# A graph network on one core: loads between layers 0 and 1 that wait for rows of y

## The chip, the cores and the metric

The kernel runs on one core of one Trainium2 chip. The metric is device time in microseconds, from launch to end, as the median of several runs. Times inside a run come from one profiled execution and are counted from the start of its span.

## The reference

2708 nodes with 512 features each pass through four layers. Each layer normalises the features (LayerNorm), computes something over the adjacency matrix and adds it to x. Layer 0 is a weighted mean over neighbours. Layer 1 is an attention whose mask is so strong that the kernel reduces it to a choice of one row: for each node, the row of the projected matrix y that the largest entry of the node's adjacency row points to. Layer 2 is a two-step graph convolution and layer 3 a mean over neighbours.

```python
h = relu(layernorm(x));  x = x + layer0(h, adj)
h = relu(layernorm(x));  x = x + layer1(h, adj)        # here: x1 + y[idx]
h = relu(layernorm(x))
h = relu(adj @ (h @ W1) + b1)
h = relu(adj @ (h @ W3) + b3)
x = x + tanh(h @ Wf + bf)
h = relu(layernorm(x));  x = x + (adj != 0) @ (h @ W + b) / deg
```

## The kernel before

Nodes are cut into 22 tiles of 128 rows (the last has 20). Matrices are split into high, low and shifted parts, so that each product in layer 2 is three products at the fast float32 rate. The adjacency is treated as dense in its first six column tiles; beyond them, each node tile has a list of the neighbours that occur, and the rows of those are gathered by indirect transfers. Only node tile 0 reads the whole adjacency column.

Layer 0 leaves two things in device memory: x1, its output in tiles, and y, the projected rows that layer 1 picks from. The core then opens the passage to layer 2. `fetch(t)` (L1034) loads tile t of x1 on SyncE's queue and gathers the rows `y[idx]` on GpSimd's queue; slots are there for nine tiles (AHEAD, L1032), and nine fetches are issued at the start (just above L1074). `first_product(t)` (L1047) adds the two, stores x2, normalises, calls `fetch(t + 9)`, transposes and splits (`relu_parts`, L871), multiplies by W1 (`project3`, L889), and stores the product in g1d. The main loop of this step (L1077) goes over node tiles m. For each, `aggregate` (L943) loads its list (`load_listed`, L926), gathers listed rows of g1d, and loads pieces of three adjacency tiles (`load_piece`, L915) that are marked (L953) and split by ScalarE (L971) and VectorE (L972, L973). For m = 0 the pieces cover all 22 tiles, and calling for their parts is what drives `first_product` through t = 0 to 21. The gathers of g1d for m = 1 need all 22 products stored.

Weights pass through one raw buffer `wr`: W3 is split from it right after the nine fetches (L1074), Wf is loaded into it at once (L1075), and inside the loop at m = 0 it is split into the space of W1, and W is loaded. The biases b1 and b3 are loaded ahead of the fetches (L1027, L1028).

The order on each engine isn't the order of the program text. The framework's scheduler places every instruction by its own idea of durations, and semaphores carry the dependences. Each engine then works through its list strictly in order, SyncE's and GpSimd's transfer issues included. So where an instruction stands is fixed when the kernel is built, and one that waits holds all that stand behind it on its engine.

A helper `behind(dst, last)` existed in layer 0 only: it copies one element on VectorE from a tile into the buffer that a load is about to fill. The load overwrites that buffer and so can't be issued before the copy, and the copy can't run before its source is there.

Of the kernel before, what the change touches and what calls it, by code (L numbers as in the profile page):

```python
# [9 lines left out]
FP = mybir.dt.float32  # L10
# [12 lines left out]
P = 128  # L23
# [19 lines left out]
def kernel(  # L43
# [27 lines left out]
    nc = tc.nc  # L71

    N, D = x.shape
    H, _, DK = wk_d.shape
    NT = (N + P - 1) // P
    NFULL = N // P
# [10 lines left out]
    def rows(t):  # L87
        return min(P, N - t * P)

    def dense_of(m):  # L90

        return 0 if m == NT - 1 else DENSE
# [59 lines left out]
    def span(t):  # L152
        return slice(t * P, t * P + rows(t))

    def project(acc, hT, n, w):

        for c in range(NCD):
            nc.tensor.matmul(  # L158
                acc[:n], hT[:, c, :n], w[:, c, :], start=(c == 0), stop=(c == NCD - 1)
            )  # L160

    def load_w(pool, src, name, first=None):
        w = pool.tile([P, NCD, D], FP, name=name)
        if first:
            first(w)
        nc.sync.dma_start(out=w, in_=src.rearrange("(c p) k -> p c k", p=P))
        return w
# [23 lines left out]
    def split_b(hi, lo, s, v, scale=1.0):  # L191

        nc.scalar.activation(hi, v, AF.Copy, scale=UP * scale)
        if scale == 1.0:
            nc.vector.tensor_tensor(lo, v, hi.bitcast(FP), ALU.subtract)
        else:
            nc.vector.scalar_tensor_tensor(
                lo, v, scale, hi.bitcast(FP), op0=ALU.mult, op1=ALU.subtract
            )
        nc.vector.scalar_tensor_tensor(  # L200
            s, lo.bitcast(FP), SHIFT, hi.bitcast(FP), op0=ALU.mult, op1=ALU.add
        )
        nc.scalar.activation(lo, lo.bitcast(FP), AF.Copy, scale=-SHIFT)

    def split_w(pool, raw, tag):

        w = [pool.tile([P, NCD, D], FR, name=f"{tag}{i}") for i in range(3)]
        for c in range(NCD):
            split_b(*(part[:, c, :] for part in w), raw[:, c, :])
        return w  # L210

    short = ctx.enter_context(ExitStack())
    wset = short.enter_context(tc.tile_pool(name="wset", bufs=1))
# [6 lines left out]
    with tc.tile_pool(name="l0_slab", bufs=2) as slabs, tc.tile_pool(  # L220
        name="l0_h", bufs=1
    ) as hp, tc.tile_pool(name="l0_w", bufs=2) as wp, tc.tile_pool(
        name="l0_acc", bufs=2, space=PSUM
    ) as ps_acc, tc.tile_pool(name="l0_small", bufs=1, space=PSUM) as ps_small, tc.tile_pool(
        name="l0_list", bufs=3, space=PSUM
    ) as ps_list, tc.tile_pool(name="l0_tr", bufs=1, space=PSUM) as ps_tr, tc.tile_pool(
        name="l0_y", bufs=1, space=PSUM
# [189 lines left out]
        def norm_h0(ts):  # L417
            for t in ts:
                n = rows(t)
                norm(wp, h0[t], n, h0[t], AF.Relu)  # L420
                nc.gpsimd.dma_start(out=h0d[span(t)], in_=h0[t][:n])

        def behind(dst, last):

            nc.vector.tensor_copy(dst, last)

        wv = wset.tile([P, NCD, D], FP, name="wa0")
        wo = wset.tile([P, NCD, D], FP, name="wa1")
# [49 lines left out]
        masks, row, slab = {}, {}, {}  # L478
# [277 lines left out]
        incs, hns, xs = {0: incidence(0)}, {}, {}  # L756
# [9 lines left out]
        for m in range(NT):  # L766
# [45 lines left out]
            if m == NT // 2 + 6:  # L812
                wr = load_w(wset, w1_d, "wr", lambda w: behind(w[:1, 0, :1], xt[:1, :1]))
                w1 = split_w(wset, wr, "wa")
                wr = load_w(wset, w3_d, "wr")
# [12 lines left out]
    gp = short.enter_context(tc.tile_pool(name="g", bufs=1))  # L828
    wsetb = short.enter_context(tc.tile_pool(name="wsetb", bufs=1))
    ap = short.enter_context(tc.tile_pool(name="ap", bufs=2))  # L830
    wp = short.enter_context(tc.tile_pool(name="wp", bufs=2))
# [27 lines left out]
    def sum_banks(dst, main, mixed, n):  # L859

        nc.scalar.activation(dst[:n], main[:n], AF.Copy, scale=1.0 - EPS12)
        nc.vector.scalar_tensor_tensor(  # L862
            dst[:n], mixed[:n], EPS12, dst[:n], op0=ALU.mult, op1=ALU.add
        )
# [6 lines left out]
    def relu_parts(v, n):  # L871

        pt = ps_t.tile([P, NCD, P], FP, name="pt")
        for c in range(NCD):
            nc.tensor.transpose(pt[:, c, :n], v[:n, c * P : (c + 1) * P], ident[:n, :n])  # L875
        hi, lo, s = (
            wp.tile([P, NCD, P], FR, name=f"v_{part}") for part in ("hi", "lo", "s")
        )
        d = (slice(None), slice(None), slice(0, n))
        nc.scalar.activation(hi[d], pt[d], AF.Relu, scale=UP)  # L880
        nc.vector.scalar_tensor_tensor(  # L881
            lo[d], pt[d], 0.0, hi[d].bitcast(FP), op0=ALU.max, op1=ALU.subtract
        )
        nc.vector.scalar_tensor_tensor(
            s[d], lo[d].bitcast(FP), SHIFT, hi[d].bitcast(FP), op0=ALU.mult, op1=ALU.add
        )
        return hi, lo, s

    def project3(parts, n, w, pool=None, names=("main", "mixed")):  # L889

        hi, lo, s = parts
        whi, wlo, ws = w
        main, mixed = ((pool or ps_p).tile([P, D], FP, name=name) for name in names)
        for acc, a, b, first, last in (
            (main, hi, whi, True, False),
            (main, lo, wlo, False, True),
            (mixed, s, ws, True, True),
        ):
            for c in range(NCD):
                nc.tensor.matmul(  # L900
                    acc[:n],
                    a[:, c, :n],
                    b[:, c, :],
                    start=first and c == 0,
                    stop=last and c == NCD - 1,
                )
        return main, mixed
# [4 lines left out]
    if TAIL:  # L912
        others.append([NFULL])

    def load_piece(m, ts):  # L915
        n, k = rows(m), rows(ts[0])
        raw = ap.tile([P, PIECE, P], FP, name="raw", bufs=3)
        nc.sync.dma_start(
            out=raw[:k, : len(ts), :n],
            in_=adj_t[ts[0] * P : ts[0] * P + k * len(ts), m * P : m * P + n].rearrange(  # L920
                "(t p) m -> p t m", p=k
            ),
        )
        return raw[:k, : len(ts), :n], k

    def load_listed(m):  # L926
        ac = ap.tile([P, NCA, P], FP, name="ac")[:, : CHUNKS[m], : rows(m)]
        nc.sync.dma_start(out=ac, in_=listed[m])
        return ac

# [75 lines left out]
    def aggregated(m, parts, shifted, gd, bias, marked=False):  # L1006
        n = rows(m)
        u = wp.tile([P, D], FP, name="u")
        main, mixed = aggregate(m, parts, shifted, gd, marked)
        if dense_of(m):  # L1010
            sum_banks(u, main, mixed, n)
            nc.vector.tensor_add(u[:n], u[:n], bias[:n])
        else:
            nc.vector.scalar_tensor_tensor(
                u[:n], mixed[:n], EPS12, bias[:n], op0=ALU.mult, op1=ALU.add
            )
        return relu_parts(u, n)
# [1 line left out]
    def g_parts(t):  # L1019
        return [gp.tile([P, D], FR, name=f"g{part}{t}") for part in ("hi", "lo", "s")]  # L1020

    def load_bias(src, name):
        row = wsetb.tile([P, D], FP, name=name)
        nc.sync.dma_start(out=row, in_=src.unsqueeze(0).to_broadcast([P, D]))
        return row

    bias1 = load_bias(b1_d, "bias0")  # L1027
    bias3 = load_bias(b3_d, "bias1")  # L1028


    xs, ys, g1, g1p = {}, {}, {}, {}
    AHEAD = 9  # L1032

    def fetch(t):  # L1034

        n = rows(t)
        xs[t] = gp.tile([P, D], FP, name=f"slot{t % AHEAD}")
        nc.sync.dma_start(out=xs[t][:n], in_=x1[t][:n])
        ys[t] = gp.tile([P, D], FP, name=f"slot{AHEAD + t % AHEAD}")
        nc.gpsimd.indirect_dma_start(  # L1040
            out=ys[t][:n],
            out_offset=None,
            in_=y[:, :],
            in_offset=bass.IndirectOffsetOnAxis(ap=idx[:n, t : t + 1], axis=0),
        )
# [26 lines left out]
    for t in range(min(AHEAD, NT)):  # L1072
        fetch(t)
    w3 = split_w(wsetb, wr, "wb")  # L1074
    wr = load_w(wset, wf_d, "wr")  # L1075

    for m in order_m:  # L1077
        n = rows(m)
        parts = aggregated(m, first_parts, first_product, g1d, bias1, marked=True)
        if m == 0:  # L1080
            wf = split_w(wset, wr, "wa")
            wr = load_w(wset, w_d, "wr")
        main, mixed = project3(parts, n, w3)
        go = wp.tile([P, D], FP, name="go")
        sum_banks_scaled(go, main, mixed, n)
        nc.sync.dma_start(out=g2d[span(m)], in_=go[:n])

    bf = load_bias(bf_d, "bias0")
    bl = load_bias(b_d, "bias2")

    g2, g2p, x3 = {}, {}, {}

# [153 lines left out]
    for m in order_2:  # L1246
        n = rows(m)
        parts = aggregated(m, second_parts, second_product, g2d, bias3)
        if m == 0:
            w = split_w(wsetb, wr, "wb")  # L1250
# [40 lines left out]
    AHEAD = 3  # L1291
# [32 lines left out]
    with tc.If(general > 0):  # L1324

        with tc.tile_pool(name="l0_g", bufs=2) as gp, tc.tile_pool(
            name="l0_gh", bufs=1
# [53 lines left out]
        with tc.tile_pool(name="l1_qkv", bufs=1) as qkvp:  # L1381
# [6 lines left out]
            with tc.tile_pool(name="l1_pw", bufs=1) as pwp, tc.tile_pool(  # L1388
                name="l1_ph", bufs=2
            ) as php, tc.tile_pool(name="l1_px", bufs=3) as pxp, tc.tile_pool(  # L1390
                name="l1_pps", bufs=2, space=PSUM
# [43 lines left out]
            with tc.tile_pool(name="l1_bias", bufs=2) as bp, tc.tile_pool(  # L1435
                name="l1_p", bufs=2
            ) as pp, tc.tile_pool(name="l1_pT", bufs=3) as ptp, tc.tile_pool(
                name="l1_x", bufs=1
            ) as xp, tc.tile_pool(name="l1_st", bufs=4) as stp, tc.tile_pool(
                name="l1_s", bufs=2, space=PSUM  # L1440
            ) as ps_s, tc.tile_pool(name="l1_t", bufs=2, space=PSUM) as ps_t, tc.tile_pool(
                name="l1_o", bufs=1, space=PSUM
# [84 lines left out]
        with ExitStack() as gen:  # L1527

            atp = gen.enter_context(tc.tile_pool(name="at", bufs=2))
            wp = gen.enter_context(tc.tile_pool(name="wp", bufs=3))  # L1530
# [5 lines left out]
            gp = l2.enter_context(tc.tile_pool(name="g", bufs=2))  # L1536
# [5 lines left out]
            w = load_w(wts, w_d, "w")  # L1542
# [3 lines left out]
            bf, bl = (wts.tile([P, D], FP, name=name) for name in ("bf", "bl"))  # L1546
# [74 lines left out]
            g1 = gp.tile([P, NT, D], FP, name="g")  # L1621
# [22 lines left out]
            for block in range(NB):  # L1644
# [3 lines left out]
                xs = {}  # L1648
# [38 lines left out]
            for block in range(NB):  # L1687
# [4 lines left out]
                xs = {}  # L1692
# [57 lines left out]
```

## Time and profile before

| What | us |
|---|---|
| median of the runs | 1506.5 (1505.83, 1506.5, 1511.4) |
| profiled execution, its own time | 1444.13 |
| its span, first to last instruction | 1442.3 |
| PE busy | 1294.6 |
| VectorE busy | 942.6 |
| ScalarE busy | 692.4 |
| GpSimd busy | 670.7 |
| last store of y issued | 475.3 |
| first gather of y issued | 478.38 |
| first product of layer 2 on PE | 491.8 |
| first gathered row tile of g1d used by PE | 604.45 |

The page gives the busy time of each engine, then the span in 40 slices of 36 us, in tenths. The profiled execution is 62 us shorter than the median of the runs. Lines are those of the kernel before. PE is TensorE, DVE is VectorE, ACT is ScalarE, POOL is GpSimd, and SP is SyncE, which issues transfers only.

### The profile page before, as it was taken

What the parts mean: (1) busy time and instruction counts of PE and PEld (TensorE: products, weight loads), DVE (VectorE), ACT (ScalarE), POOL (GpSimd) and SP (SyncE); (2) the same over time, 40 slices, a digit from 0 to 9 for tenths busy, and PEclk for the clock granted to TensorE, in tenths of its full rate; (3) what the DMA queues carried; (4) which work ended last, traced back from release to release, by engine and by line L of the source; (5) the groups of instructions that cost most, each with busy time, mean ns of one, the idle gap of its engine ahead of it and who ended that gap; (6) DMA issues with size and microseconds to landing.
All of it is one profiled execution on the core that took longest, in us unless ns stands there. A gap on an engine that the chain in (4) does not pass through costs nothing. (4 is left out here: it accounts for less than half of the span.)

```text
span 1442.3 us, 15447 instructions
## 1 busy us (share of the span) xinstructions
PE 1294.6 (90%) x4400; PEld 767.3 (53%) x4400; DVE 942.6 (65%) x1916; ACT 692.4 (48%) x1054; POOL 670.7 (47%) x690
## 2 busy tenths in 40 slices
PE   3889888999788499899999998999999999688997
PEld 1334333444333366556656664666677666466664
DVE  5597988999898687533434454665666666465574
ACT  8776636542562465323333342445444554354443
POOL 2154667777545320364444432333433445067762
PEclk9999999999899799999999999999999999788998
DMA  9999899998974884587777768555565657378884
GB/s 361 343 307 320 260 340 321 333 283 271 364 291 142 292 276 164 184 274 244 231 221 247 235 223 286 170 180 161 182 186 165 212 180 220 117 238 260 255 260 146
DMA packets 196188, 351.46 MB, mean 244 GB/s; under 512 B 26482, under 2 KB 107940, under 8 KB 192361
## 3 DMA queue, kind: packets, MB, share of 16 engines
q1 hardware_dynamic: 148701, 200.87, 41.3%
q0 software_dynamic: 47392, 149.51, 32.8%
q8 instruction: 37, 0.61, 0.2%
q14 instruction: 58, 0.48, 0.1%
HBM read 287.00 MB, written 63.29 MB: 243 GB/s over the span
## 5 line engine op out<-in xcount | busy, mean ns | idle before, releaser
L987 PE MATMUL aggs<-gg,ac 128*128 128x512 f32 (+1 forms) x520 | 232.3, 594 | 3.5 <-DMA gg<-g1d,idx_g 3.5
L935 POOL DMA_INDIRECT gg<-g2d,idx_g x130 | 131.0, 1008 | 217.7 <-PE aggs L987 169.4
L935 POOL DMA_INDIRECT gg<-g1d,idx_g x130 | 132.5, 1019 | 173.7 <-PE aggs L987 104.1
L562 POOL DMA_INDIRECT ac<-in_adj_t_dram,idx_a x130 | 133.6, 1027 | 96.3 <-issue 33.8
L778 PE MATMUL acc<-h,inc 128*128 128x512 f32 (+1 forms) x348 | 165.0, 616 | 7.1 <-DVE inc L630 7.0
L987 PEld LDWEIGHTS aggs<-gg,ac 128*128 128x128 f32 (+1 forms) x520 | 97.5, 189 | 110.3 <-issue 101.7
L580 POOL DMA_INDIRECT h<-h0d,idx_g x111 | 110.1, 992 | 50.7 <-issue 22.9
L971 ACT ACTIVATE a_hi<-raw 128x384 fp32r<-128x384 f32 x84 | 43.6, 520 | 160.2 <-issue 88.4
L984 PE MATMUL agg<-ghi,a_hi 128*128 128x512 f32 x252 | 114.8, 455 | 4.7 <-ACT a_hi L971 2.5
L778 PEld LDWEIGHTS acc<-h,inc 128*128 128x128 f32 (+1 forms) x348 | 65.4, 197 | 83.0 <-issue 70.9
L984 PE MATMUL agg<-glo,a_lo 128*128 128x512 f32 x252 | 101.9, 404 | 0.0
L158 PE MATMUL yacc<-wvo,hT 128*128 128x512 f32 (+1 forms) x176 | 88.9, 650 | 14.4 <-ACT hT L189 14.4
L778 PE MATMUL acc<-h,incl 128*128 128x512 f32 (+1 forms) x222 | 100.7, 600 | 0.0
L984 PE MATMUL aggs<-gs,a_s 128*128 128x512 f32 x252 | 100.1, 400 | 0.6 <-DVE gs L200 0.6
L935 POOL DMA_INDIRECT gg<-hidr,idx_h x79 | 80.1, 1013 | 44.1 <-issue 13.1
L972 DVE TENSOR_TENSOR a_lo<-raw,a_hi 128x384 fp32r<-128x384 f32 x84 | 47.2, 562 | 76.7 <-ACT a_hi L971 53.9
L881 DVE SCALAR_TENSOR_TENSOR v_lo<-pt,v_hi 128x512 fp32r<-128x512 f32 (+1 forms) x88 | 56.7, 665 | 45.9 <-ACT v_hi L880 45.6
L862 DVE SCALAR_TENSOR_TENSOR u<-aggs,u 128x512 f32<-128x512 f32 x42 | 28.9, 687 | 76.4 <-PE aggs L987 74.8
L510 ACT ACTIVATE sgn<-ar 128x2708 bf16<-128x2708 f32 (+1 forms) x22 | 54.0, 2455 | 35.2 <-DMA ar<-in_adj_dram 35.2
L880 ACT ACTIVATE v_hi<-pt 128x512 fp32r<-128x512 f32 (+1 forms) x88 | 48.8, 578 | 44.2 <-PE pt L875 42.3
L778 PEld LDWEIGHTS acc<-h,incl 128*128 128x128 f32 (+1 forms) x222 | 42.0, 191 | 52.5 <-issue 45.6
L158 PEld LDWEIGHTS yacc<-wvo,hT 128*128 128x128 f32 (+1 forms) x176 | 34.2, 202 | 60.9 <-issue 38.2
(285 smaller groups left out, 2822.2 us busy)
## 6 DMA issues: line engine op xcount, KB each, us to landing
ar<-in_adj_dram SPq DMA_DIRECT2D x27, 1354.0 KB
raw<-in_adj_t_dram SPq DMA_DIRECT2D x108, 192.0 KB
slot<-x SPq DMA_DIRECT2D x41, 256.0 KB
at<-in_adj_t_dram SPq DMA_DIRECT2D x27, 384.0 KB
ranks<-rank_b SPq DMA_DIRECT2D x20, 485.0 KB
ac<-lst SPq DMA_DIRECT2D x16, 384.0 KB
h<-in_x_dram SPq DMA_DIRECT2D x21, 256.0 KB
h0d<-h POOLq DMA_DIRECT2D x21, 256.0 KB, 5.7
```

The source lines that it names most:

```text
L158: nc.tensor.matmul(acc[:n], hT[:, c, :n], w[:, c, :], start=(c == 0), stop=(c == NCD - 1))
L510: nc.scalar.activation(sgn[:n], ar[:n], AF.Sign, accum_out=sum_sgn[:n])
L562: nc.gpsimd.indirect_dma_start(out=ac[:, c, :n], out_offset=None, in_=adj_units, in_offset=bass.IndirectOffsetOnAxis(ap=idx_a[:, m, c0 + c ...
L580: nc.gpsimd.indirect_dma_start(out=g, out_offset=None, in_=h0d[:, :], in_offset=bass.IndirectOffsetOnAxis(ap=idx_g[:, m, c : c + 1], axis=0),)
L778: nc.tensor.matmul(acc[:n], a, g, start=(i == 0), stop=(i == len(pairs) - 1))
L880: nc.scalar.activation(hi[d], pt[d], AF.Relu, scale=UP)
L881: nc.vector.scalar_tensor_tensor(lo[d], pt[d], 0.0, hi[d].bitcast(FP), op0=ALU.max, op1=ALU.subtract)
L935: nc.gpsimd.indirect_dma_start(out=gs[c], out_offset=None, in_=gd[:, :], in_offset=bass.IndirectOffsetOnAxis(ap=index[:, m, c : c + 1], ax ...
L971: nc.scalar.activation(hi[d], raw, AF.Copy, scale=UP)
L972: nc.vector.tensor_tensor(lo[d], raw, hi[d].bitcast(FP), ALU.subtract)
L984: nc.tensor.matmul(acc[:n], a[:k, i, :n], b[:k], start=st, stop=sp)
L987: nc.tensor.matmul(mixed[:n], a, g, start=(c == 0 and not dense_of(m)), stop=(c == len(chunks) - 1),)
```

## The change

`behind` moves to the outer level, and loads in the passage are made to wait with it:

- x1 tile t, from t = 2 on, waits for the gathered tile t - 2 of y. The y slot is now named ahead of the load.
- A one-column tile `landed` is copied from the gathered tile 0 of y. The adjacency pieces and lists of m = 0 and m = 1, and the biases b3 and b, wait for it. b3 is loaded after the nine fetches instead of ahead of them.
- Wf is no longer loaded ahead of the loop, but at m = 0, and waits for `g1[NFULL]`, the product of the last node tile. Its split and the load of W follow it as before.

```diff
+    not_before = []
+
     def load_piece(m, ts):
         n, k = rows(m), rows(ts[0])
         raw = ap.tile([P, PIECE, P], FP, name="raw", bufs=3)
+        for last in not_before:
+            behind(raw[:1, 0, :1], last[:1, :1])
         nc.sync.dma_start(
...
     def load_listed(m):
         ac = ap.tile([P, NCA, P], FP, name="ac")[:, : CHUNKS[m], : rows(m)]
+        for last in not_before:
+            behind(ac[:1, 0, :1], last[:1, :1])
         nc.sync.dma_start(out=ac, in_=listed[m])
...
-    def load_bias(src, name):
+    def load_bias(src, name, last=None):
         row = wsetb.tile([P, D], FP, name=name)
+        if last is not None:
+            behind(row[:1, :1], last)
         nc.sync.dma_start(out=row, in_=src.unsqueeze(0).to_broadcast([P, D]))
...
-    bias3 = load_bias(b3_d, "bias1")
...
+    SOON = 2
+
     def fetch(t):
         n = rows(t)
         xs[t] = gp.tile([P, D], FP, name=f"slot{t % AHEAD}")
+        ys[t] = gp.tile([P, D], FP, name=f"slot{AHEAD + t % AHEAD}")
+        if t >= SOON:
+            behind(xs[t][:1, :1], ys[t - SOON][:1, :1])
         nc.sync.dma_start(out=xs[t][:n], in_=x1[t][:n])
-        ys[t] = gp.tile([P, D], FP, name=f"slot{AHEAD + t % AHEAD}")
         nc.gpsimd.indirect_dma_start(
...
     w3 = split_w(wsetb, wr, "wb")
-    wr = load_w(wset, wf_d, "wr")
+    landed = wp.tile([P, 1], FP, name="landed", bufs=1)
+    behind(landed[:1], ys[0][:1, :1])
+    bias3 = load_bias(b3_d, "bias1", landed[:1])
     for m in order_m:
         n = rows(m)
+        not_before[:] = [landed] if m < 2 else []
         parts = aggregated(m, first_parts, first_product, g1d, bias1, marked=True)
         if m == 0:
+            wr = load_w(wset, wf_d, "wr", lambda w: behind(w[:1, 0, :1], g1[NFULL][:1, :1]))
             wf = split_w(wset, wr, "wa")
             wr = load_w(wset, w_d, "wr")
...
-    bl = load_bias(b_d, "bias2")
+    bl = load_bias(b_d, "bias2", landed[:1])
```

## The prediction

> **What bounds the kernel now.** I read the page first: the span and the slices.
>
> ```profile
> span 1442.3 us, 15447 instructions
> PE 1294.6 (90%) x4400; PEld 767.3 (53%) x4400; DVE 942.6 (65%) x1916; ACT 692.4 (48%) x1054; POOL 670.7 (47%) x690
> PE   3889888999788499899999998999999999688997
> PEclk9999999999899799999999999999999999788998
> DMA  9999899998974884587777768555565657378884
> ```
>
> PE is busy for 90% of the span, so a change pays only where PE stands idle. The 14th digit of the PE row is a 4: that slice (36 us long, from 469 us) is the passage between the layers, where the clock digit falls to 7. So I cut the passage into stretches (columns: length, busy time and count of each engine, granted clock, DMA share, GB/s).
>
> ```profile
> 475.00:490.00 15.00, 0.00 (x1) 0.01 (x1) 9.48 (x21) 6.09 (x12) 9.18 (x9) 0.61 0.89 314
> 490.00:525.00 35.00, 29.33 (x119) 22.31 (x119) 28.78 (x67) 23.56 (x45) 6.77 (x8) 0.87 0.90 316
> 525.00:592.00 67.00, 66.29 (x282) 46.36 (x282) 51.58 (x120) 35.21 (x70) 6.82 (x7) 1.00 0.55 177
> 592.00:620.00 28.00, 24.44 (x80) 14.32 (x79) 13.63 (x24) 8.49 (x17) 19.21 (x18) 0.94 0.73 238
> ```
>
> PE loses 15.0 us before its first product, 35 - 29.3 = 5.7 us in the ramp, 0.7 us in the steady part and 3.6 us where node tile 1 waits for its gathered rows. Only the first two can be a gain. The timeline of POOL, DVE, PE and ACT names the waits (start, length, instruction, idle before and what ended it):
>
> ```profile
> 478.38 0.99 POOL L1040 DMA_INDIRECT slot<-y,idx  x1 [10.10 <-DMA bias<-in_L_gnn_b_dram]
> 485.51 0.69 DVE L1052 TENSOR_TENSOR slot<-slot,slot 128x512 f32<-128x512 f32 x1 [4.61 <-DMA slot<-y,idx]
> 490.00 1.11 PE L875 MATMUL pt<-ident,slot 128*128 128x128 f32 x4 [15.38 <-ACT slot L182]
> 498.59 0.52 ACT L953 ACTIVATE nz<-raw 128x384 uint8<-128x384 f32 x1 [1.71 <-DMA raw<-in_adj_t_dram]
> 499.65 1.19 PE L900 MATMUL agg<-wa,v_hi 128*128 128x512 f32 x4 [2.30 <-ACT v_hi L880]
> 514.90 0.50 PE L984 MATMUL agg<-ghi,a_hi 128*128 128x512 f32 x1 [1.95 <-ACT ghi L193]
> 518.32 1.16 ACT L953 ACTIVATE nz<-ac 128x1152 uint8<-128x1152 f32 x1 [1.80 <-DMA ac<-lst]
> 604.45 1.95 PE L987 MATMUL aggs<-gg,ac 128*128 128x512 f32 x2 [3.52 <-DMA gg<-g1d,idx_g]
> ```
>
> The first gather of y is issued at 478.38 and lands at 485.5, 7.1 us later; over all 22 gathers, issue to landing is 3.8 us at the least, 6.2 in the median, 7.4 at most. The stretches from 482 to 496 show a DMA share of 0.99 to 1.06: the gathers queue behind nine tiles of x1, two biases and Wf. ACT, in order, then stops on a raw piece that was issued at 488.7 and is there only at 498.6, and takes PE with it (2.30 us).
>
> **What the Trainium skill says.** "DMA: Bandwidth & Descriptors", section "Issuing engines are not separate DMA queues": transfers begun by SyncE and by GpSimd run on the same 16 engines and interleave. The trace agrees: 3.8 us against 7.1 us for the same gather at a share above 1. The same page, "Anatomy of one DMA", prices a transfer at 2.0 us plus bytes over 436 GB/s: 2.6 us for 256 KB, an estimate; the trace's 3.8 us is used instead. "TensorE: Matmul & The Clock Gate", Part 1: an idle window of about 3.4 us halves the clock, and a busy one as long restores it. The trace agrees: 0.50 from 480 to 494, full again by 496. "VectorE: DVE Perf Modes", the errata section, prices a one-element operation at 58 + 1 cycles of 0.96 GHz, 0.06 us; the 1x1 copies that exist show 0.13 us each, begun about 0.07 apart. I use the trace.
>
> **The change, part by part.** The built order of the changed program differs from before only from the passage to the end of node tile 1; POOL's order is the same throughout.
>
> (1) *Loads taken out of the crowd.* b3 (256 KB) and Wf (1024 KB) leave the stretch from 475 to 496, and x1 tiles 2 to 8 go out one by one as y lands. 1.25 MB at the 390 GB/s of that stretch is 3.2 us of all engines. I give the first gather 4.0 us (from 3.8 to 7.1), so y0 lands at 482.4 and not at 485.5: 3.1 us earlier.
>
> (2) *What the copies hold up.* They sit in DVE's in-order queue. In the built order the shift of tile 0, which releases ACT's norm and PE's first transpose, stands behind the copies that wait for y1, y2, y3 and y4, and behind the addition that waits for the late x1 tile 2. POOL issues y4 at 483.96, because its gathers are 1.25 us apart; with 3.8 to 4.6 us it lands at 487.8 to 488.6. The shift runs at about 488.4 instead of 488.90. So of the 3.1 us, 0.5 us arrives at PE; bounds -1.5 (a landing of 6 us) to +1.
>
> (3) *The ramp.* Three things are better. The built order has the transposes of tile 1 ahead of the products of tile 0, the raw piece comes through emptier queues, and the wide lists (640 and 576 KB, loaded at 507 to 512 before) come some 60 us later. The 2.3 us before tile 1 go. Of the rest, 0.64 and 1.95 us idle and an estimated 1.5 us from a clock of 0.83 between 510 and 520, I take half: 2.0 us. Sum 4.3; bounds 0 to 7. DVE caps it: 43 operations of 0.6 us (25.8), some 5 us of small ones and copies, and 4 us of forced waits from 482.4 put the sixth tile's last step near 517, against 524.4 before.
>
> (4) *Later copies.* 35 one-element copies are added: 20 for x1, 11 for pieces and lists of m = 0 and 1, one for landed, three for b3, b and Wf. At 0.07 to 0.13 us each that is 2.5 to 4.6 us of DVE, spread over 110 us. From 525 to 592 DVE is busy 51.6 of 67 us and PE 66.3, so PE covers it: 0.3 us. If that cover were gone, the 4.6 would show. Each copy also waits: x1 tile t for the landing of y t-2 and for the store of x2 t-9 out of the same slot. Behind it stand go, v_lo and v_s of the current tiles, and PE waits for those. Most have slack. The copy for tile 13 has not: y11 can be gathered only after tile 2's transposes (about 499), so it lands near 504 while v_s of tile 3 is queued behind it. I take 1.5 us for all such stalls; bounds 0 to 12 (0.6 us at each of 20).
>
> (5) *What is moved late.* The two lists are now read by ACT around tile 18. Their marks stopped ACT for 0.8 and 1.8 us before; ACT has gaps there, PE none, so 1.0 us (0 to 4). Wf is issued behind the last store of g1d, at about 593.7, and lands about 598; its split was run from 590 to 599, when ACT and DVE had room, and W follows it. ACT and DVE wait for Wf at a time when PE waits for gathers anyway. But Wf's 1 MB shares the queues with them (share 1.02 to 1.08 from 600 to 606): 1.0 us, from 0 to the 2.7 us that 1 MB takes at 390 GB/s. SP passes the Wf issue to the end and gains nothing else.
>
> Sum: -0.5 - 4.3 + 0.3 + 1.5 + 1.0 + 1.0 = -1.0 us; I round to -1.5, since the late stalls overlap with waits that PE has anyway. The profiled execution took 1444.13 us, 1.8 us around its span of 1442.3; it becomes about 1442.6. The runs without a profile have a median of 1506.5, 62 us more, for which the trace has no place; I carry the difference over: 1505.0.
>
> **The rivals.** *A, the passage gains and the copies and moved loads give most of it back:* 1505.0, between 1500 and 1511. For it: the gather's wait and the raw wait are seen; against it nothing but the sizes.
> *B, the ramp is recovered whole:* all 5.7 us of idle, 1.5 us of clock and 1.5 us at the start, with late costs near 0: -8.5, 1498. For it: DVE too stands idle for 6.2 of the 35 us of the ramp, much of it behind ACT's stops for late transfers. Against it: the shift of tile 0 behind y4.
> *C, slower: the copies at the head of DVE's queue.* Its place is the stretch from 490 to 592. Before, a late y tile held only its own addition; now it holds every step behind the copy. Gathers took 4.6 to 6.5 us after 507. The price is 0.6 us at each of 20 copies, 12 us, against 4.8 of gain, with 2 us of late loads: +9, 1515.5. It decides from a mean stall of 0.14 us, (4.8 - 2)/20, where the gain is gone. Against it: y t-2 is asked for seven tiles ahead of its use.
> *D, the loads stay in each other's way:* each landing frees an x1 load of the same size every 1.25 us, 420 GB/s with the gather, more than the 390 seen. The gathers then land as late as now and the rest cancels: 1506.5.
>
> **How the numbers follow.** A 0.50, D 0.26, B 0.12, C 0.12. Half a per cent, 7.5 us, is about what a measurement of this kernel can tell from no change (its three runs spread over 5.6 us). Below 1499 lies most of B and little of A: faster 0.11. Above 1514 lies most of C and little of D: slower 0.12. The rest is 0.77. The range takes A and D, and the nearer part of B and C: 1498 to 1513.
>
> **What would show it.** In the changed profile: the first addition of y at 482 to 483, not 485.5; PE's first transpose at 489 to 490; transposes of tile 1 ahead of tile 0's products and no wait of 2.3 us; DVE waiting at the new copies for under 3 us in all; PE idle in the ramp under 4 us; the gathers of g1d at the end of the passage up to 1 us later in their stretch. Wrong would be DVE copies with 5 us or more of waits, PE idle between 525 and 592 above 3 us, or a first gather that still takes 7 us.

## The result

The changed kernel takes 1506.22 us (median of 19 runs, 1498.7 to 1515.19) and the kernel before 1506.5 us (19 runs, 1495.66 to 1516.62): a ratio of 1.0004, with a 95% interval of 0.9982 to 1.0027. No difference can be seen. Sets of runs made together lie at one of two levels, whatever the program, 1434 to 1456 us or 1494 to 1518 us. The profile of before is of the lower level and that of after of the upper one; its page:

```profile
span 1499.8 us, 15498 instructions
PE 1313.2 (88%) x4400; PEld 772.1 (51%) x4400; DVE 947.8 (63%) x1951; ACT 693.3 (46%) x1054; POOL 672.6 (45%) x690
PE   3879797879968579989999999899999999678987
PEclk9979898889979889999999999999999999888999
DMA  9978897896887487487767777656555656476875
```

The 57 us by which its span is longer are not the change's: the first gather of y is issued at 515.34 and not at 478.38, behind code of layer 0 that nothing touches. Everything below is therefore counted from that gather. The four stretches of before, moved by 36.96 us, in the changed kernel (same columns):

```profile
511.96:526.96 15.00, 0.00 (x0) 0.00 (x0) 8.10 (x20) 4.37 (x9) 9.15 (x9) 0.56 0.54 171
526.96:561.96 35.00, 28.46 (x116) 20.59 (x116) 30.45 (x79) 21.72 (x40) 6.66 (x6) 0.89 0.81 272
561.96:628.96 67.00, 63.37 (x268) 44.98 (x266) 52.59 (x140) 36.41 (x68) 7.59 (x7) 1.00 0.63 204
628.96:656.96 28.00, 23.14 (x71) 11.40 (x71) 12.14 (x22) 9.49 (x19) 14.87 (x15) 0.88 0.77 255
```

The DMA share of the first stretch fell from 0.89 to 0.54: the crowd is gone. PE gained nothing from it there. In the third stretch, where PE stood still for 0.7 us, it now stands still for 3.6. The timeline tells why:

```profile
515.34 1.28 POOL L1053 DMA_INDIRECT slot<-y,idx  x1 [10.37 <-ACT wb L207]
519.05 0.14 DVE L164 COPY slot<-slot 1x1 f32<-1x1 f32 x1 [1.96 <-DMA slot<-y,idx]
527.32 0.14 DVE L164 COPY slot<-slot 1x1 f32<-1x1 f32 x1 [3.36 <-DMA slot<-y,idx]
528.85 0.14 DVE L164 COPY slot<-slot 1x1 f32<-1x1 f32 x1 [0.67 <-DMA slot<-y,idx]
528.92 0.19 DVE L183 TENSOR_SCALAR shift<-mv,rstd 128x1 f32<-128x1 f32 x1
530.02 2.20 PE L875 MATMUL pt<-ident,slot 128*128 128x128 f32 x8 [19.33 <-ACT slot L186]
536.15 0.14 DVE L164 COPY slot<-slot 1x1 f32<-1x1 f32 x1 [1.38 <-DMA x<-slot]
539.48 0.52 ACT L960 ACTIVATE nz<-raw 128x384 uint8<-128x384 f32 x1 [1.12 <-DMA raw<-in_adj_t_dram]
585.48 0.14 DVE L164 COPY slot<-slot 1x1 f32<-1x1 f32 x1 [1.71 <-DMA slot<-y,idx]
650.15 1.90 PE L994 MATMUL aggs<-gg,ac 128*128 128x512 f32 x2 [2.44 <-DMA gg<-g1d,idx_g]
```

y0 is seen 3.7 us after its gather, where it took 7.1. But the shift of tile 0 (L183) needs a reciprocal whose input ACT has ready by 523.8; on DVE the reciprocal stands behind the copy for y3 and the shift behind that for y4. It runs 13.6 us after the gather (before: 10.5), and PE starts 3.1 us later. PE's first eight transposes are those of tiles 0 and 1, and the wait of 2.30 us is gone.

### The profile page after: what moved, and what is told of

Read it like the earlier page. It is cut to its first block, busy times and chain, and to the rows that moved or that the text cites. A ratio compares the mean times of both kernels' runs of the same rounds, so it can differ in the third digit from the quotient of the medians.

```text
span 1499.8 us, 15498 instructions
## 1 busy us (share of the span) xinstructions
PE 1313.2 (88%) x4400; PEld 772.1 (51%) x4400; DVE 947.8 (63%) x1951; ACT 693.3 (46%) x1054; POOL 672.6 (45%) x690
## 4 chain that ended last, share of the span: by engine, by line
PE 53%; DMA 5%; DVE 3%; issue 2%; ACT 2%; another core or an unknown queue 0%; POOL 0%; SPq 0%; ACTq 0%; DVEq 0%; POOLq 0%
PE aggs L994 14%; PE main L900 9%; PE agg L991 7%; PE mixed L900 4%; PE agg L1188 4%; PE aggs L991 4%; PE aggs L1188 3%; PE pt L875 3%; DMA raw<-in_adj_t_dram 1%; PE main L1188 1%; DMA slot<-y,idx 1%; PE aggs L1006 1%; PE agg L900 1%; PE mixed L1188 1%; DMA glo<-hid 1%
## 5 line engine op out<-in xcount | busy, mean ns | idle before, releaser
L562 POOL DMA_INDIRECT ac<-in_adj_t_dram,idx_a x130 | 128.2, 986 | 107.8 <-DMA lst<-ac 39.0
L580 POOL DMA_INDIRECT h<-h0d,idx_g x111 | 118.2, 1064 | 73.6 <-PE acc L778 35.9
L158 PE MATMUL yacc<-wvo,hT 128*128 128x512 f32 (+1 forms) x176 | 96.1, 695 | 38.6 <-issue 20.9
L862 DVE SCALAR_TENSOR_TENSOR u<-aggs,u 128x512 f32<-128x512 f32 x42 | 28.9, 687 | 82.2 <-PE aggs L994 65.0
```

Source lines behind the costliest of these rows:

```text
L158: nc.tensor.matmul(acc[:n], hT[:, c, :n], w[:, c, :], start=(c == 0), stop=(c == NCD - 1))
L562: nc.gpsimd.indirect_dma_start(out=ac[:, c, :n], out_offset=None, in_=adj_units, in_offset=bass.IndirectOffsetOnAxis(ap=idx_a[:, m, c0 + c ...
L580: nc.gpsimd.indirect_dma_start(out=g, out_offset=None, in_=h0d[:, :], in_offset=bass.IndirectOffsetOnAxis(ap=idx_g[:, m, c : c + 1], axis=0),)
```

## The experiments

The one measure of all runs is PE's *lost time*: the length of a slice less PE's busy time in it times the granted clock, summed over slices of 5 to 10 us. It counts idle time and halved clock alike. Each row is one execution; other slices move the column 115 to 140 by up to 0.7 us, the others hardly at all. The stretches are counted from the first gather of y; the column 140 to 170 stands apart, because in some executions of the upper level it holds a stall that no row explains (e5, below).

| execution | level | y0 seen | shift of tile 0 | 0-20 | 20-40 | 40-115 | 115-140 | sum to 140 | 140-170 |
|---|---|---|---|---|---|---|---|---|---|
| before | lower | 7.1 | 10.5 | 15.5 | 4.8 | 1.1 | 4.9 | 26.3 | 0.1 |
| before again, e1 | lower | 7.1 | 10.5 | 15.5 | 5.6 | 1.4 | 6.0 | 28.5 | 0.1 |
| after | upper | 3.7 | 13.6 | 16.8 | 2.2 | 5.0 | 6.2 | 30.2 | 1.0 |
| after again, e2 | lower | 4.9 | 13.0 | 16.7 | 2.6 | 6.3 | 4.6 | 30.2 | 1.1 |
| after, timed, e9 | lower | 3.5 | 11.3 | 14.3 | 4.8 | 6.5 | 5.6 | 31.2 | 3.3 |
| x1 not tied, e3 | lower | 6.6 | 9.9 | 15.3 | 1.7 | 3.9 | 5.1 | 26.0 | 0.1 |
| x1 not tied, timed, e10 | lower | 6.8 | 10.1 | 15.7 | 2.5 | 3.8 | 6.9 | 28.9 | 0.2 |
| x1 tied alone, e5 | upper | 7.1 | 10.8 | 14.6 | 3.7 | 4.0 | 5.5 | 27.8 | 8.1 |
| x1 tied alone, timed, e12 | upper | 7.5 | 11.0 | 15.1 | 5.2 | 5.1 | 6.4 | 31.8 | 6.8 |
| biases and Wf late alone, e6 | upper | 6.8 | 10.1 | 15.6 | 3.4 | 2.6 | 6.5 | 28.1 | 1.8 |
| pieces and lists late alone, e7 | upper | 8.0 | 11.4 | 15.7 | 5.3 | 2.4 | 4.3 | 27.7 | 7.4 |
| tied to y t-5, e8 | upper | 3.9 | 11.0 | 16.7 | 4.6 | 2.6 | 5.1 | 29.0 | 3.0 |
| b3 later still, e4 | lower | 4.0 | 12.0 | 14.7 | 3.4 | 5.7 | 4.7 | 28.5 | 0.6 |
| tied once, e11 | lower | 3.6 | 9.6 | 15.4 | 5.2 | 5.1 | 4.5 | 30.2 | 1.2 |

**My theory** after the result: the gathers do come earlier, but each new copy is a wait at the head of DVE's queue, and this takes the gain back, first at tile 0's shift and then in the middle. **The rivals**: the differences of the two traces are scatter; b3, loaded in the middle of the gathers, makes y3 and y4 late; or the late lists and Wf cost it, not the copies.

**e1 and e2: is the passage a property of the program?** Both kernels again, without an edit.

> The kernel before, once more, to see how far the passage scatters from one execution to the next. All times are counted from the issue of the first gather of y. In the profile shown: y0 has landed at 7.1 us, the shift of tile 0 runs at 10.5, PE's first transpose at 11.6, tile 5's last step ends at 46.0, tile 21's at 115.6, the first product with gathered rows of g1d is at 126.1, node tile 2's last step ends at 161.4. If these are a property of the program (my theory: the passage of the changed kernel can be compared step by step), they repeat within 1 us up to the ramp and within 2 us to the end. If the passage scatters as the rest of the kernel does (rival: the differences of 3 to 5 us between the two profiles are scatter), they move by 3 us or more.

> The changed kernel once more. Counted from the issue of the first gather of y, its profile has y0 seen at 3.7 us, y3 and y4 7.9 us after their own issues, the shift of tile 0 at 13.6, PE's first transpose at 14.7, tile 5's last step at 44.7, tile 21's at 119.5, the first gathered product at 127.3, node tile 2's last step at 166.8. Theory (a property of the program): the shift again between 12.5 and 14.5, y3 late again, PE starts 2 to 4 us later than before and still ends tile 5 up to 2 us earlier. Rival (scatter): the shift lies near 10 us, y3 lands 4 us after its issue.

e1 repeats the shift to 0.01 us, tile 5's last step to 1.0 us (47.05), the first gathered product to 1.3 (127.3), and is off by 2.2 at node tile 2 (163.5). e2 has the shift at 13.0 and node tile 2 at 166.5. In the aligned 67 us of the third stretch PE is idle for 0.7 and 0.8 us before, and for 3.6, 4.9 and 5.1 in the three executions of the changed kernel, at both levels. The third of these (e9) has the shift at only 11.3 us, so the late start scatters by 2.3 us; the loss in the middle does not go away. It is no scatter.

**e3: the copies for x1 left out.**

```
-        if t >= SOON:
-            behind(xs[t][:1, :1], ys[t - SOON][:1, :1])
```

> The changed kernel without the copies that tie x1 tile t to y t-2: biases, pieces, lists and Wf stay late. Theory (the shift of tile 0 stands on DVE behind copies that wait for y1 to y4): the shift now waits only for y0 to y2; all nine tiles of x1 go out at once, so y0 is seen at 4 to 7 us, but the shift runs at 8 to 10 us instead of 13.6 and PE's first transpose at 9 to 11. Rival (the gathers land late for a reason of their own, the copies hold nothing up): the shift stays at 12 us or later.

```profile
485.48 0.14 DVE L164 COPY landed<-slot 1x1 f32<-1x1 f32 x1 [4.82 <-DMA slot<-y,idx]
488.80 0.19 DVE L183 TENSOR_SCALAR shift<-mv,rstd 128x1 f32<-128x1 f32 x1
489.89 1.12 PE L875 MATMUL pt<-ident,slot 128*128 128x128 f32 x4 [15.50 <-ACT slot L186]
```

The first gather was issued at 478.89. y0 is seen 6.6 us later, much later than in the changed kernel, and yet the shift runs at 9.9 and PE starts at 11.0. So in the changed kernel the landing of y0 is not what PE's start waits for; the copies ahead of the shift on DVE are, as the theory said. The ramp keeps its gain (1.7 instead of 5.2); the middle still loses 3.9.

**e4: b3 with Wf, behind the last g1.**

```
-    bias3 = load_bias(b3_d, "bias1", landed[:1])
+            bias3 = load_bias(b3_d, "bias1", g1[NFULL][:1, :1])
```

(The added line stands ahead of Wf's load at m = 0.)

> The changed kernel with b3 loaded behind the last g1 together with Wf, and not as soon as y0 has landed; everything else as changed. b3 is one row of 2 KB read 128 times; where b1 and b3 are under way, the trace shows a DMA share of 0.4 to 0.6 and 80 to 180 GB/s, beside 1.0 and 390 GB/s in the stretches next to them. Theory (that load slows the gathers y3 to y5, which land 7.7 to 7.9 us after their issues): they land 4 to 5 us after their issues, the shift of tile 0, still behind the copy for y4, runs at 9.5 to 11 us instead of 13.6 and PE's first transpose at 10.5 to 12. Rival (the landings free one x1 load each, and these crowd the gathers, b3 or not): y3 and y4 land 7 us or more after their issues, the shift stays at 13 us.

y3 and y4 land 6.4 and 6.0 us after their issues, and the shift is at 12.0: neither what the theory said (4 to 5) nor the rival (7 or more). The changed kernel's own executions have 7.9 and 7.9, 6.6 and 6.1, 5.9 and 5.8, so the run lies within their scatter. That b3 delays the gathers falls as an explanation of size; whether it adds some tenths stays open.

**e5 to e7: one part of the change at a time.** In e5 only the copies for x1 are kept (SOON = 2), in e6 only the late b3, b and Wf, in e7 only the late pieces and lists; the rest is as before. In short:

```
e5: +        if t >= SOON:
    +            behind(xs[t][:1, :1], ys[t - SOON][:1, :1])
e6: +    bias3 = load_bias(b3_d, "bias1", landed[:1])
    +            wr = load_w(wset, wf_d, "wr", lambda w: behind(w[:1, 0, :1], g1[NFULL][:1, :1]))
    +    bl = load_bias(b_d, "bias2", landed[:1])
e7: +        not_before[:] = [landed] if m < 2 else []
```

> The kernel before with one part of the change alone: x1 tile t is tied to the landing of y t-2; biases, pieces, lists and Wf are loaded as before. The measure is PE's lost time by stretch, counted from the issue of the first gather of y: the length of a slice less PE's busy time in it times the granted clock. Before, in two executions: 0 to 20 us 15.5 and 15.5, 20 to 40 4.8 and 5.6, 40 to 115 1.1 and 1.4, 115 to 140 4.9 and 6.0, 140 to 170 0.1 and 0.1, sum 26.4 and 28.6. Changed: 16.8 and 16.7, 2.2 and 2.6, 5.0 and 6.3, 6.2 and 4.6, 1.0 and 1.1, sum 31.1 and 31.3. Changed without these copies: 15.3, 1.7, 3.9, 5.1, 0.1, sum 26.1. Theory (the copies, waiting at the head of DVE's queue, are what takes the gain back, and cost 3 to 5 us wherever they are): start 16 to 18, ramp 4 to 6, middle 2.5 to 4, sum 29.5 to 32. Rival (they cost something only beside the other parts, or their own gain of free queues pays for them): start 15.5 or less, middle under 2, sum 28.5 or less.

> The kernel before with b3 behind y0, b behind y0 and Wf behind the last g1; x1 not tied, pieces and lists as before. Measure as in the run with the copies alone. Theory (the 3 us that the ramp gains come from the wide lists and Wf leaving the crowd, and the middle loses 2.5 us of it since ACT stops at lists that come late): without the lists' part the ramp gains about half, 3 to 4.5, and the middle keeps the 1.1 to 1.9 of before; sum 25 to 27.5. Rival (Wf late is what disturbs the middle): middle above 2.5.

> The kernel before with the pieces and lists of node tiles 0 and 1 behind the landing of y0; x1 not tied, biases and Wf as before. Measure as in the run with the copies alone. Theory: the ramp gains, 2 to 4 instead of 5.2, and the middle shows what the lists' late arrival costs, 2.5 to 4.5 instead of 1.2, so that the sum stays within 1 us of before, 26.5 to 28.5. Rival (the lists cost nothing in the middle): middle under 2 and sum 25 to 26.

The middle behaves roughly as a sum. Before loses 1.25 us there on average; the copies alone add 2.7 (e5, and 3.8 in e12), b3, b and Wf alone 1.3, pieces and lists alone 1.1. With the 1.25 of before that is 6.4 to 7.5; the changed kernel has 5.0 to 6.5. So late b3, b and Wf do disturb the middle in this one execution, as the rival of e6 has it (above 2.5; 2.6), and the lists cost a little less than the theory of e7 says; the copies are the largest part. The start refutes me: with the copies alone it is 14.6 and 15.1, not 16 to 18, and the sum of e5, 27.8, is the rival's; only with the tied x1 and a late b3 together is it ever above 16. In the ramp I had it the wrong way round as well: the late lists gain nothing (5.3), the late biases and Wf do (3.4), and both together more (1.7 and 2.5).

The 8.1 us of e5 behind 140 us are something else:

```profile
667.09 0.52 ACT L978 ACTIVATE a_hi<-raw 128x384 fp32r<-128x384 f32 x1 [18.53 <-remote]
669.21 1.22 PE L900 MATMUL main<-wb,v_hi 128*128 128x512 f32 x2 [4.75 <-ACT v_hi L880]
```

"remote" means that the profile finds no releaser. No such wait ends within the first 140 us of any run. The longest, in e5 and e7, begin at about 129 us, but the column 115 to 140 is no higher there than elsewhere, so I compare the sums up to 140 us across the levels.

**e8: tied to a gather farther back.**

```
-    SOON = 2
+    SOON = 5
```

> The changed kernel with one size changed: x1 tile t is tied to y t-5 instead of y t-2. Tiles 0 to 4 of x1 are then free, and in the built order the shift of tile 0 stands behind the copies for y1, y2 and y3, no longer behind that for y4; later copies ask for a y that was gathered five tiles before and has landed long ago. Theory (the stalls at the copies are the cost): shift of tile 0 at 11 to 12.5 us from the first gather instead of 13.0 to 13.6, lost time in the start 15.5 to 16.5, in the middle 3 to 4.5 instead of 5.0 to 6.3, copies' waits for y from 60 us on gone, sum 27 to 29.5 instead of 31.2. Rival (not the copies' waits but the changed order of the instructions costs it): middle 5 or more, sum 30.5 to 32.

The shift is at 11.0 and the middle loses 2.6: both better than expected. No copy waits for a y after the first 11 us, and PE's idle time in the aligned third stretch is 1.2 us, against 3.6 to 5.1 with y t-2 and 2.0 without the copies. So the waits for y are gone with the nearer tie. But 1.2 us is less than with no copies at all, so the order of the instructions has changed the stretch as well. The start (16.7) and the ramp (4.6) did not improve. The sum to 170 us, 32.0, is the rival's, though some of its last 3.0 us follows a wait of DVE without a releaser (2.88 us). The trace shows a second wait, which the prediction named and the theory of this run left out:

```profile
542.05 0.14 DVE L164 COPY slot<-slot 1x1 f32<-1x1 f32 x1 [3.24 <-DMA x<-slot]
542.97 2.08 PE L900 MATMUL mixed<-wa,v_s 128*128 128x512 f32 x4 [2.79 <-DVE slot L164]
```

The copy for tile 9 of x1 also waits for the store of x2 tile 0 out of the same slot. Before, only the load on SP waited for that; now DVE does, with v_s of the tile in work behind it, and PE with it.

**e9 and e10: does it reach the end?** The changed kernel and the kernel of e3, both timed.

> The changed kernel, timed beside the one before on the same chip in five rounds. In the trace the passage of the changed kernel is longer: counted from the last store of y, the last step of node tile 2 ends 4.2 to 6.3 us later than before (170.6 and 170.8 against 164.4 and 166.4), and PE's lost time in it is 31.2 us against 27.5. Theory (the passage's loss reaches the end of the program): 3 to 6 us slower, a ratio of 1.002 to 1.004. Rival (it is taken back later, or the executions where the two were compared were no fair pair): within 1.5 us, a ratio of 0.999 to 1.001, as the first result says, 1.0004.

> The changed kernel without the copies that tie x1 tile t to y t-2, timed. PE's lost time in the passage was 26.1 us with these copies left out, against 27.5 before and 31.2 changed. Theory (the copies cost 5 us of the passage, and take back what the other parts gain): 0 to 3 us faster than before, ratio 0.998 to 1.000, and 4 to 6 us faster than the changed kernel. Rival (the copies make no difference that reaches the end): within 1.5 us of the changed kernel.

Both sets lie at the lower level, beside a before of 1444.85 us. Changed: 1447.72 us, ratio 1.0023 (1.0003 to 1.0044), about 3.3 us slower. Without the copies: 1444.44 us, ratio 1.0007 (0.9989 to 1.0025), neither faster nor slower. (The ratios are the recorded ones, which are not the quotients of the medians.) The two medians differ by 3.3 us, and over the 22 runs of each, made in one set, the means differ by 3.7 us, with a 95% interval of 0.9 to 6.4 if the runs are taken as independent. So the copies cost time as well as lost time, by an amount that is poorly known. The trace of e9 shows one link whole:

```profile
546.01 0.14 DVE L164 COPY slot<-slot 1x1 f32<-1x1 f32 x1 [1.89 <-issue]
546.08 0.19 DVE L183 TENSOR_SCALAR shift<-mv,rstd 128x1 f32<-128x1 f32 x1
546.31 0.82 ACT L186 ACTIVATE slot<-slot,shift,rstd 128x512 f32<-128x512 f32 x1 [2.59 <-DVE shift L183]
549.89 1.21 PE L900 MATMUL main<-wa,v_hi 128*128 128x512 f32 x4 [1.97 <-ACT v_hi L880]
553.93 0.14 DVE L164 COPY slot<-slot 1x1 f32<-1x1 f32 x1 [1.57 <-DMA slot<-y,idx]
559.10 1.12 PE L1006 MATMUL aggs<-go,raw 128*128 128x512 f32 x2 [1.07 <-DVE go L869]
```

DVE stops for 1.89 us at a copy; the shift behind it is late, ACT waits for the shift, and PE in the end waits 1.97 us. The same link is in e2 (1.88 and 1.98) and in none of the kernels without the copies. For the 1.89 us the profile names no releaser ("issue"). The copy is that of tile 19, whose y17 was asked for 6.5 us before, and with the tie moved back to y t-5 (e8) the wait is gone; so I take it for the landing of y17. The next stop, 1.57 us at the copy of tile 21, is for a y by name, and PE waits 1.07 us soon after it.

Not all of the middle is the copies'. At 45 to 53 us from the gather PE has three waits, of 0.90, 0.69 and 0.69 us, for ACT, and such waits are there without the copies, too, at 42 to 51 us (e3):

```profile
521.32 0.50 PE L991 MATMUL agg<-ghi,a_hi 128*128 128x512 f32 x1 [0.92 <-ACT ghi L197]
523.37 1.20 PE L900 MATMUL main<-wa,v_hi 128*128 128x512 f32 x4 [0.69 <-ACT v_hi L880]
529.07 1.10 PE L1006 MATMUL aggs<-go,raw 128*128 128x512 f32 x2 [0.80 <-DVE v_lo L881]
```

Those make 2.3 us in each execution of the changed kernel, and 2.4 and 2.3 in e3 and e10. What follows the copies' stops at 64 and 72 us is 1.2 us after the change, 2.8 in e2 and 3.0 in e9, and nothing in e3 and e10.

**e11: one tie and no more.**

```
-        if t >= SOON:
-            behind(xs[t][:1, :1], ys[t - SOON][:1, :1])
+        if 3 <= t < AHEAD:
+            behind(xs[t][:1, :1], ys[0][:1, :1])
```

> The changed kernel with the tie done once: x1 tiles 3 to 8 wait for the landing of y0, tiles 0 to 2 are free, and from tile 9 on nothing is tied; biases, lists and Wf late as changed. No step of tile 0 then stands on DVE behind a gather later than y2. Theory (early gathers come through empty queues, and the price of the change is the chain of waits on DVE): y0 seen at 4 to 5 us from the first gather, the shift of tile 0 at 7.5 to 9.5, PE's first transpose at 8.6 to 10.6; lost time in the start 13.5 to 14.5 instead of 16.8, in the middle 2.5 to 4 instead of 5.0 to 6.3, sum 24 to 26; time 2 to 4 us under before, ratio 0.997 to 0.999. Rival (the six x1 tiles that go out at y0's landing crowd y1 and y2, which lose what y0 gains): shift at 10 us or later, sum 27 or more, time within 1.5 us of before.

y0 is seen at 3.6 us, the shift is at 9.6 and PE starts at 10.7, the earliest of all. It is no gain: 1445.54 us, ratio 1.0018 (1.0000 to 1.0037), lost time 30.2. Early gathers are worth one microsecond at PE's start, and the ramp loses 5.2 us, as it did before. One wait stands out there, 2.39 us for ACT, which had stopped for the second raw piece:

```profile
497.33 0.52 ACT L960 ACTIVATE nz<-raw 128x384 uint8<-128x384 f32 x1 [2.94 <-DMA raw<-in_adj_t_dram]
500.66 0.11 DVE L164 COPY raw<-landed 1x1 f32<-1x1 f32 x1
501.27 0.38 SPq L923 DMA_DIRECT2D raw<-in_adj_t_dram  x1
507.26 0.52 ACT L960 ACTIVATE nz<-raw 128x384 uint8<-128x384 f32 x1 [2.53 <-DMA raw<-in_adj_t_dram]
508.77 0.50 PE L991 MATMUL agg<-glo,a_lo 128*128 128x512 f32 x1 [2.39 <-ACT glo L207]
```

That piece goes out at 24.8 us from the gather (before: 21.6). Its tie is to y0, which had landed at 3.6, but the copy that holds the load stands some 20 us farther back in DVE's order, and SP can issue the load only after it. So a marker can delay a load by its place alone, with no wait to be seen at it. It does not explain the whole ramp: in e3 and e10 ACT waits 5.4 and 7.0 us for raw pieces, against 5.5 here, and the ramp loses only 1.7 and 2.5.

So the theory is true of the copies, but not enough: taking most of their waits away (3.6 us of DVE are left, for 13 to 15) did not give the time back here. The build also orders each of these programs anew, and no run holds the order fixed while only a wait changes. How much of e11's 5.1 in the middle is order and how much late pieces stays open.

**e12: the copies alone, timed.** The kernel of e5.

> The kernel before with the copies that tie x1 tile t to y t-2 and nothing else of the change, timed. Its single look was on a chip whose trace has waits of ACT and DVE that no row explains. Theory (the copies are the price, whatever stands beside them): lost time in the passage 30 to 33 us against 26.4 and 28.6 before, with 2.5 us or more of it in the middle (40 to 115 us from the first gather), where before has 1.1 and 1.4; time 2 to 5 us above before, ratio 1.0015 to 1.0035. Rival (the copies cost only beside late lists and Wf): lost time 29 us or less, middle under 2, ratio 0.999 to 1.001.

1508.47 us beside a before of 1504.28, ratio 1.0018 (0.9991 to 1.0045); lost time 31.8 to 140 us, middle 5.1. The trace is where the theory put it; the time has the sign it said, but its interval includes 1.

## Why the prediction came out right

The time is within 1.3 us of the 1505.0 that I gave, and rival A, gain and loss that cancel, is what the first result looks like. That closeness is in part luck. The sum behind it, -1.5 us, has the wrong sign in the trace, and two of my three signs of being wrong are there: copies with far more than 5 us of waits, and PE idle for 3.6 us where I had set the limit at 3. The number survived because what I had missed is 3 us, which the measurement at the upper level cannot tell from nothing, and because the runs of the changed kernel came at the same level as those of before.

1. *Loads taken out of the crowd*: held. y0 is seen 3.5 to 4.9 us after its gather; I had said 4.0.
2. *What the copies hold up*: right mechanism, wrong size. I had the shift 0.5 us earlier, with bounds of -1.5 and +1. It is 0.8 to 3.1 us later (11.3, 13.0 and 13.6 against 10.5), because y3 and y4 took 5.8 to 7.9 us and not 3.8 to 4.6. The step took the best landing for all gathers, but the x1 loads that the first landings free run beside y3 and y4: the DMA share is 1.0 again from 10 us on. That these loads are what slows them is argued from the share; no run takes them alone away. Rival D, which said this of all gathers, was right from y3 on.
3. *The ramp*: mostly held. The 2.3 us are gone, and tile 5's last step ends 44.7 to 45.2 us after the gather, 46.0 and 47.0 before, although PE starts later. Lost time in the ramp is 3.2 us on average against 5.2: 2.0, where I gave 4.3, and one of the three executions (e9, 4.8) has next to none of it.
4. *Later copies*: the copies' own time is as small as said, 0.14 us each. Their waits were mis-sized: 13 to 15 us of DVE in all, 5.2 to 8.2 behind the first 15 us, where I had said under 3 in all. (1.9 to 3.3 of them are the wait for y0, for which DVE had waited 4.61 before.) In the middle the copies cost PE 2.1 us (5.9 against 3.85 without them), for my 1.5. The copy for tile 13 that I singled out is not where it fell (0.2 to 1.1 us, where it shows); the waits for the slot's store at tiles 9 and 11, and those at tiles 19 and 21 some 64 and 72 us in, are.
5. *Moved late*: the lists cost 1.1 us alone (e7), as I said. Wf among the gathers costs nothing that shows: the stretch from 115 to 140 loses 5.5 us on average before and changed. The one wait of 3.52 us for gathered rows has become several (2.44 us at 650.15 and 1.74 soon after), and some of it falls after 140 us, where the changed kernel loses 1.0 to 3.3 us for 0.1. With Wf as late and no copies it loses 0.1 and 0.2 there (e3, e10), so that is not Wf's.

In sum I had -1.0 us. The passage up to 140 us loses 30.5 us on average for 27.4, so +3.1. Counted to 170 us, at the lower level, it is 31.3 and 34.5 (e2, e9) for 26.4 and 28.6. It is with the copies that this comes and goes: without them the average to 140 us is 27.5 (e3, e10), with them alone 29.8 (e5, e12), and the last step of node tile 2 ends 161.1 and 163.5 us after the gather without them, 161.4 and 163.5 before, 166.5 to 169.1 changed. How much of it is their waits and how much the order and the later loads that come with them stays open, because e11, with few waits, loses 30.2 as well.

The first gather is also issued later after the last store of y (4.0 to 4.2 us for 2.9 and 3.1). In the changed kernel b1's load goes out on SP ahead of that store, but that is not shown to be the reason: in e8 the store goes first and it is 4.4 us, and one and the same kernel has 3.8 (e3) and 2.9 (e10).

At the lower level the time agrees: +3.3 us (0.4 to 6.4). At the upper level it is +0.6 (-2.7 to +4.1); the two intervals overlap. So rival C was there, at DVE's queue: DVE stood for 12 to 14 us at the 20 copies for x1, as C had it, but PE covered most of that, and the passage grew by 3.1 us. A's gain, 2.0 us in the ramp, paid for part of the 5.1 lost in the start and the middle, not for most of it. C's "decides from a mean stall of 0.14 us" was passed.

The 62 us between profile and median, which I carried over, are the distance between the two levels and have nothing to do with profiling: at the lower level the runs of before have a median of 1444.85 us, as its profile had 1444.13.

## What to carry to other kernels

A dependence that is to hold back a load is paid for by the engine that carries it, not by the queue that issues the load: ask what stands behind the marker in that engine's order, whether it waits for the buffer's old reader as well, and how late its own place in the order lets the load go. Tie to something that landed long ago, not to what has just been asked for: with y t-5 in place of y t-2 PE's idle time in the steady stretch fell from between 3.6 and 5.1 us to 1.2 (2.0 with no tie), although the passage as a whole lost 29.0 us, for 30.2 to 31.2. And an earlier landing is worth only what the next engine's order lets through; 3.4 us at the gather became less than nothing at PE.

## What the runs showed of the hardware

An empty queue did not make the first gather fast. In e2 the first gather is issued at 481.88, takes POOL 2.31 us to issue, and has the queues to itself; the window from 475 to 500 us in 40 slices of 0.625 us:

```profile
DMA  0079656410000002765797889868999999999998
GB/s 0 7 203 341 266 154 174 134 46 0 0 0 0 0 0 52 197 210 131 256 118 243 324 269 229 161 203 269 403 390 413 413 393 361 331 361 380 403 308 308
```

For six slices, from 480.6 to 484.4, nothing moves: 2.5 us after the issue begins there is still no transfer. y0 is seen at 486.76, 4.9 us after the issue. The least that any of these executions has for y0 is 3.5 us.

The two levels: the kernel before took 1437.08 us in one set and 1504.28 (median) in another. At the upper level the profiles have waits with the releaser "remote", 69 to 113 us of ACT and 25 to 54 us of DVE in each; at the lower level there are none. What they wait for, no run here shows.
